# A four-layer network on one core: the order of work in the Mamba's opening, and a group norm cut into stages in the attention

## The chip, the cores and the metric

The kernel runs on one NeuronCore of a Trainium2 chip. A core has five engines that run side by side and wait for each other by semaphores: TensorE (matrix products, written to the PSUM memory), VectorE, ScalarE (activation functions, from tables that have to be loaded), GpSimd, and SyncE, which here only issues DMA transfers. In the profile they are PE (PEld for its weight loads), DVE, ACT, POOL and SP. [...] The metric is the device time of one execution in microseconds, as a median of several runs; lower is better.

## The reference

An image batch `x` of 2 × 128 channels × 56 × 56 pixels goes through four layers. Each has the form `x = x + layer(group_norm(x))`, the norm over 32 groups of 4 channels:

```
x = x + agent_attention(_gn(x))   # layer 0
x = x + conv3x3(_gn(x))           # layer 1
x = x + mixture_of_experts(_gn(x))# layer 2: 2x2 patches, 8 experts, the best 2 of each patch
x = x + mamba_pair(_gn(x))        # layer 3
```

Layer 0 replaces queries by mixtures of 49 agent vectors and then lets each of the 3136 pixels attend to all others, in 4 heads: `softmax(q_compressed @ k.T * scale) @ v`, then a projection and a layer norm. Layer 3 runs, over each image row of 56 pixels, a state-space recurrence forward and one backward. For each way:

```
xi, z = split(x @ in_w.T)
xc  = silu(conv_b + causal_conv4(xi))
dt, B, C = split(xc @ xproj_w.T)            # 8, 16 and 16 values per pixel
dt  = softplus(dt @ dt_w.T + dt_b)          # 256 channels
h_t = exp(dt_t * A) * h_(t-1) + (dt_t * xc_t) * B_t     # 16 states per channel
y   = (sum over states of h * C + xc * D) * silu(z)
```

The group norm itself: per channel a mean and a variance over the pixels, averaged over the four channels of a group, then `(x - mean) / sqrt(var + eps)`.

## The kernel before, in words

Everything is float32. The image stays in on-chip memory as `x[128, 2, 3136]` and is worked on in 7 blocks of 448 pixels per image (8 rows of 56). A version of the attention that is safe for extreme values stands behind a branch at the end and isn't entered for these inputs.

**The group norm** is a method of `Net`. VectorE has taken statistics of every block (`bn_stats`, L88). `group_norm` aggregates them (L94, `gn_mv`), has TensorE average them over groups by a product with a constant matrix (L96), fetches the means and forms a corrected variance (L98 to L102, `gn_q`), averages that over groups by a second product (L104), and takes the inverse root (`inverse_root`, L66 to L71): an addition on VectorE, Ln and Exp on ScalarE, three small VectorE operations.

**The attention** (`short_attention`) is a list of 14 blocks, image 0 and then image 1, each with 25 steps (key tiles of 128 pixels). Step i of a block computes the scores of one key tile for four heads (L584, `sc`), their exponentials (L587, `ex`, two ScalarE instructions of 128 × 896), adds these into a running sum on VectorE (L592 and L594, `ex_sum`), and multiplies an earlier tile's exponentials with the values (L602, `av`). `den` (L622) adds the sums up. The order on TensorE, ScalarE and VectorE is the order in which the program writes the instructions (`manual_schedule`). Besides, each step has room for one stage of other work. At fixed steps stages finish the block before (`after`: `divide` at 3 with a reciprocal of 2.95 us, `project` at 6, `measure` at 8 and so on) or prepare the next one (`ahead`: `q_scores` at 9, `q_softmax` at 11, `q_turn` at 15, `q_mix` at 18). In the steps left over, the list `rest` is worked off, one stage a step, from step 3 on (in the first block from the start). In it is the opening of the second image: seven `stats`, `norm`, then in turn `spread` of a block (VectorE: normalise, L110, and sum for the agents, L477) and `keys` of the same block (TensorE: L508 `k_ps`, ScalarE copies it, L509), at last agents and values. A stage may return a `fetch`, which is called at the start of the next step, ahead of that step's scores. In the block before the last (`n == len(blocks) - 2`), `rest` is the convolution's group norm and the seven `pad` stages that normalise image 0 for it. All score, key and norm tiles in PSUM come from one ring of three (`ps`, tag `sc`).

**The Mamba** (`mamba_pair`) works on 14 blocks as well. Each block has a forward and a backward half of 16 units (8 pairs of states by 2 halves of the 256 channels); a unit is an exponential `dA` on ScalarE (`decay`, L1656), a product `dBu` on GpSimd (`push`, L1667), a scan on VectorE (L1689), and later a product with C (L1695 on GpSimd or L1698 on VectorE) and a sum over states on TensorE. The preparation of the next block is booked in `agenda` at numbered steps of the loop: `run(step)` emits what is booked, `fetch(step + 1)` what it returned. For block 0 the steps are negative (`at = -32`), ahead of the loop: there is nothing else to do then, and the steps only set the order. In this part only ScalarE's order is that of the program; the other engines' order is chosen by a scheduler. The stages of a half are `conv` (L1545, then ScalarE `xc`, L1554), `silu` (loads a table, applies Silu, and loads the table for Exp and Ln back), `low` (L1574, copied at L1577), `send_low` (SyncE: to memory and back, spread over partitions, as `Bs` and `Cs`), `step` (L1597, four activations L1607 to L1611), `error`, `log`, `softplus` (L1627, L1628), `weigh` (GpSimd, L1632) and `send_steps` (SyncE: `dt2` and `dtu2`, L1644). Here all their PSUM tiles share the tag `mm`, which has one buffer.

Of the kernel before, what the change touches and what calls it, by code (L numbers as in the profile page):

```python
# [8 lines left out]
F32 = mybir.dt.float32  # L9
# [19 lines left out]
class Net:  # L29
# [57 lines left out]
            self.stats[b] = self.small.tile([P, NBLK, 6], F32, name=f"st{b}", tag=f"st{b}")  # L87
        self.nc.vector.bn_stats(self.stats[b][:, k, :], self.xb(b, k))  # L88

    def group_norm(self, b, pool, tag):  # L90

        nc, small = self.nc, self.small
        mv = small.tile([P, 2], F32, name="gn_mv", tag="gn_mv")
        nc.vector.bn_aggr(mv, self.stats[b].rearrange("p k s -> p (k s)"))  # L94
        ps = pool.tile([P, 512], F32, name="gn_ps", tag=tag)
        nc.tensor.matmul(ps[:, 0:1], self.group, mv[:, 0:1], start=True, stop=True)  # L96
        mean = small.tile([P, 1], F32, name="gn_mean", tag="gn_mean")
        nc.vector.tensor_copy(mean, ps[:, 0:1])  # L98
        d = small.tile([P, 1], F32, name="gn_d", tag="gn_d")
        nc.vector.tensor_sub(d, mv[:, 0:1], mean)  # L100
        q = small.tile([P, 1], F32, name="gn_q", tag="gn_q")
        nc.vector.scalar_tensor_tensor(q, d, d, mv[:, 1:2], ALU.mult, ALU.add)  # L102
        ps2 = pool.tile([P, 512], F32, name="gn_ps2", tag=tag)
        nc.tensor.matmul(ps2[:, 0:1], self.group, q, start=True, stop=True)  # L104
        rstd = small.tile([P, 1], F32, name="gn_rstd", tag="gn_rstd")
        self.inverse_root(rstd, ps2[:, 0:1])
        return mean, rstd

    def normed(self, out, in_, mean_rstd):
        self.nc.vector.tensor_scalar(out, in_, mean_rstd[0], mean_rstd[1], ALU.subtract, ALU.mult)  # L110
# [273 lines left out]
def short_attention(net, wide, conv):  # L384
# [20 lines left out]
    with ExitStack() as ctx:  # L405
# [56 lines left out]
            net.take_stats(m.b, k)  # L462

        def norm(m):
            m.norm = net.group_norm(m.b, banks, "mm")

        def spread(m, k):

# [231 lines left out]

        def opening(m):
            todo = [lambda k=k: stats(m, k) for k in range(NBLK)]
            todo.append(lambda: norm(m))
            for k in range(NBLK):
                todo += [lambda k=k: spread(m, k), lambda k=k: keys(m, k)]
            todo += [lambda: agents_of(m), lambda: agent_products(m)]
            if m is images[0]:

                first = [getattr(blocks[0], ahead[i]) for i in sorted(ahead)]
                v = values_of(m)  # L710
                todo += [v[0], first[0], v[1], v[2], first[1], v[3], first[2], v[4], first[3]]
            else:
                todo += values_of(m)
            return todo
# [17 lines left out]
        with tc.manual_schedule(engines={E.PE, E.Activation, E.DVE}):  # L732
# [10 lines left out]
            for n, blk in enumerate(blocks):  # L743
                if n == len(blocks) - 2:
                    pad = one.tile([P, PAD * PAD], F32, name="pad0", tag="xn0")
                    rest = [lambda: conv.norm(0, banks, "mm")]
                    rest += [lambda k=k: conv.pad(0, pad, k) for k in range(NBLK)]
                for i in range(STEPS):
                    for f in fetches:
                        f()  # L750
                    fetches = []
                    blk.score(i)
                    waiting.append((blk, i))
                    quota = 0 if i == 1 else 2 if i == 3 else 1
                    if n == 0 and i == 0:
                        quota = 0
                    for _ in range(quota):
                        if len(waiting) > 1:
                            who, at = waiting.pop(0)
                            fetches.append(who.average(at))  # L760
                    if i == 2 and prev:
                        prev.sum_up(len(ENDS) - 1)
                    if i - 2 in ENDS:
                        blk.sum_up(ENDS.index(i - 2))
                    stage = None
                    if i in after and prev:
# [52 lines left out]
class Conv3x3:  # L819
# [21 lines left out]
        return [lambda some=some: turn(some) for some in (range(0, 4), range(4, 8), range(8, 9))]  # L841

    def norm(self, b, ps, tag):
        self.norms[b] = self.net.group_norm(b, ps, tag)

    def pad(self, b, pad, k):

# [538 lines left out]
def mamba_pair(net, out, wts, combine):  # L1386
# [19 lines left out]
    with ExitStack() as ctx:  # L1406
# [125 lines left out]
        class Half:  # L1532
# [101 lines left out]
                at = 0 if self.w.d == "f" else HW - 1  # L1634
                nc.gpsimd.memset(self.dt.rearrange("p m (r t) -> p (m r) t", t=HW)[:, :, at : at + 1], 1e31)

            def send_steps(self):

                self.dt2 = work.tile([P, 2, 2, BLK], F32, name="dt2", tag="dt2")
                self.dtu2 = work.tile([P, 2, 2, BLK], F32, name="dtu2", tag="dtu2")  # L1640
                for to, src in ((self.dtu2, self.dtu), (self.dt2, self.dt)):
                    for s in range(2):
                        for r in range(2):
                            nc.sync.dma_start(to[s * H : (s + 1) * H, :, r, :], src[r * H : (r + 1) * H, :, :])  # L1644

            def unit(self, u):
                return u // 2, u % 2
# [81 lines left out]
        def book(step, *stages, tag="mm", late=0):  # L1729

            agenda.setdefault(step, []).extend((stage, tag, late) for stage in stages)

        for n, blk in enumerate(blocks):
# [3 lines left out]
            if n == 0:  # L1737
                book(at + 1, blk.norm)
                for i, (h, m) in enumerate(((f, 0), (f, 1), (b, 0), (b, 1))):
                    book(at + 4 + 2 * i, lambda h=h, m=m: h.conv(m))  # L1740
                    book((1, 4, 5, 13)[i], lambda h=h, m=m: h.gate(m))
                book(at + 14, lambda f=f: silu(f, None), lambda b=b: silu(b, None))
                book(at + 16, f.low)
                book(at + 17, f.send_low)
                for h, t in ((f, at + 16), (b, 0)):
                    for m in range(2):
                        book(t + 2 + 3 * m, lambda h=h, m=m: h.step(m))
                        book(t + 3 + 3 * m, lambda h=h, m=m: h.error(m))
# [115 lines left out]
def layers(tc, a, out, wide, attention):  # L1864
    with ExitStack() as ctx:
        net = Net(ctx, tc, a)
        keep = ctx.enter_context(tc.tile_pool(name="keep2", bufs=1, side="right"))
        with tc.tile_pool(name="l1_keep", bufs=1) as taps:
# [5 lines left out]
            with tc.tile_pool(name="l2_w", bufs=2) as wpool:  # L1874
                with tc.tile_pool(name="l1_ps", bufs=2, space=PSUM) as ps, tc.tile_pool(name="l1", bufs=2) as nat:
# [3 lines left out]
                    def convolved(b):  # L1879
                        if b in done:  # L1880
                            return
                        pad = wpool.tile([P, 4, 2048], F32, name=f"pad{b}", tag="w1").rearrange("p q f -> p (q f)")
                        pad = pad[:, : PAD * PAD]
                        conv.norm(b, ps, "mm")
# [52 lines left out]
```

## Time and profile before

| | us |
|---|---|
| median of 3 runs | 3184.22 (3183.93 to 3184.84) |
| the profiled execution | 3175.44, its span 3173.7 |
| attention, up to the first product of the convolution | 0 to 902 |
| convolution, routing | 902 to 1066 |
| experts | 1066 to 1712 |
| their results gathered, Mamba's opening | 1712 to 1808 |
| Mamba loop, from its first scan to the addition after the last products | 1808 to 3141 |

Times in the profile are microseconds from the start of the span. A row of the timeline has start, duration, engine, line, operation, result and sources, and in brackets the idle time of the engine before it and what ended that. Matmuls of float32 show as two records each, so `x8` is four matmuls. A row of the waits names who waited, on which line, for whom, and then the total, the number of times and the longest. TensorE's granted clock is 1.00 at full speed.

### The profile page before, as it was taken

Reading aid. Unit: us, or ns where it says so; the run is one execution under the profiler, and the core shown is the slowest. Engines: PE = TensorE matmul, PEld = TensorE weight load, DVE = VectorE, ACT = ScalarE, POOL = GpSimd, SP = SyncE. Lnnn points to the kernel's source line nnn. Section 1 sums busy time; section 2 is a strip of 40 time slices with the busy share of each in tenths; the row PEclk is TensorE's granted clock in tenths of the full one; section 3 lists DMA queues with packets and bytes.
Section 4 is the critical chain, followed back from the end, with each engine's and each line's share of the span. In section 5 each row is a group of like instructions: output and inputs, shape, how many; then the busy total and the mean of one; then the engine's idle time right before and its main releaser. Section 6 shows DMA issues by size and latency. Waiting matters only on the chain. (4 is left out here: it accounts for less than half of the span.)

```text
span 3173.7 us, 34586 instructions
## 1 busy us (share of the span) xinstructions
PE 2863.2 (90%) x13024; PEld 1091.1 (34%) x13024; DVE 2201.9 (69%) x1985; ACT 1752.3 (55%) x2618; POOL 1411.1 (44%) x755
## 2 busy tenths in 40 slices
PE   7899999998999799999995689998898988999985
PEld 3233333332344444444442223332233332233321
DVE  5788999998854211111112389999999999999997
ACT  5678878887720111111100367777777777777764
POOL 2000010000000000000002389999999999999996
PEclk9999999999998899999997698998999999898987
DMA  1000000000001687878755434454444354445350
GB/s 53 1 1 1 1 1 1 1 1 1 1 31 27 266 323 283 324 282 322 286 228 178 103 72 95 88 104 89 92 87 101 84 107 89 85 87 108 81 111 7
DMA packets 133397, 333.65 MB, mean 105 GB/s; under 512 B 20100, under 2 KB 90596, under 8 KB 129620
## 3 DMA queue, kind: packets, MB, share of 16 engines
q1 hardware_dynamic: 111616, 304.87, 33.5%
q0 software_dynamic: 5136, 14.70, 1.4%
q10 hardware_dynamic: 16452, 11.61, 1.1%
q8 instruction: 107, 1.75, 0.2%
q14 instruction: 86, 0.70, 0.1%
HBM read 262.56 MB, written 17.20 MB: 88 GB/s over the span
## 5 line engine op out<-in xcount | busy, mean ns | idle before, releaser
L1667 POOL TENSOR_TENSOR dBu<-dtu,Bs 128x896 f32<-128x896 f32 x448 | 923.2, 2087 | 72.2 <-DVE h L1689 52.2
L1689 DVE TENSOR_TENSOR_SCAN h<-dA,dBu 128x896 f32<-128x896 f32 x448 | 878.6, 2006 | 58.1 <-ACT dA L1656 56.5
L587 ACT ACTIVATE ex<-sc 128x896 f32<-128x896 f32 (+1 forms) x700 | 602.8, 917 | 111.1 <-PE sc L584 99.9
L594 DVE TENSOR_TENSOR ex_sum<-ex_sum,ex 128x1792 f32<-128x1792 f32 (+1 forms) x238 | 490.0, 2059 | 44.1 <-ACT ex L587 30.0
L1709 PE MATMUL y<-h,both 128*64 128x448 f32 x1792 | 474.5, 631 | 15.6 <-POOL h L1695 13.0
L584 PE MATMUL sc<-q,k 32*128 32x448 f32 (+1 forms) x2800 | 403.0, 589 | 3.6 <-ACT ex L587 2.9
L1208 PE MATMUL h_ps<-w,xs_c 128*128 128x512 f32 x896 | 392.0, 595 | 10.6 <-issue 9.9
L1656 ACT ACTIVATE dA<-dt,f_A 128x448 f32<-128x448 f32 x448 | 284.4, 637 | 110.3 <-DVE h L1689 76.8
L602 PE MATMUL av<-ex,va 128*32 128x448 f32 (+1 forms) x2800 | 335.0, 553 | 0.1
L1698 DVE TENSOR_TENSOR h<-h,c_ps 128x1792 f32<-128x1792 f32 x154 | 311.3, 2022 | 25.6 <-PE c_ps L1677 10.8
L549 POOL TENSOR_TENSOR a_e<-a_e,a_inv 112x784 f32<-112x784 f32 x14 | 41.6, 2973 | 644.1 <-ACT ex L587 436.5
L1656 ACT ACTIVATE dA<-dt,b_A 128x448 f32<-128x448 f32 x448 | 283.7, 636 | 62.9 <-DVE h L1689 50.0
L1212 DVE TENSOR_TENSOR he<-h_ps,sg 128x512 f32<-128x512 f32 x56 | 38.6, 691 | 397.0 <-PE h_ps L1208 374.3
L1159 POOL DMA_INDIRECT xr<-xd,whom x28 | 28.0, 998 | 593.8 <-PE xr_ps L1198 489.2
L1695 POOL TENSOR_TENSOR h<-h,Cs 128x1792 f32<-128x1792 f32 x70 | 279.1, 3986 | 3.2 <-DVE h L1689 2.8
L1677 PE MATMUL c_ps<-low,ident 40*64 40x448 f32 x616 | 173.2, 643 | 91.4 <-DVE h L1698 69.3
L1208 PEld LDWEIGHTS h_ps<-w,xs_c 128*128 128x128 f32 x896 | 168.5, 190 | 218.6 <-issue 201.9
L1709 PEld LDWEIGHTS y<-h,both 128*64 128x64 f32 x1792 | 117.9, 152 | 319.9 <-issue 248.4
L584 PEld LDWEIGHTS sc<-q,k 32*128 32x128 f32 (+1 forms) x2800 | 137.4, 181 | 231.1 <-issue 134.8
L1229 PE MATMUL o_ps<-w,ht 128*128 128x512 f32 x448 | 200.0, 599 | 8.0 <-DMA w<-in_L_conv_w_dram 8.0
L1231 ACT ACTIVATE ot<-o_ps,share 128x512 f32<-128x512 f32 x28 | 19.2, 688 | 287.0 <-PE o_ps L1229 287.0
L1211 ACT ACTIVATE sg<-h_ps 128x512 f32<-128x512 f32 x56 | 33.4, 597 | 256.8 <-PE h_ps L1208 256.8
(318 smaller groups left out, 3007.1 us busy)
## 6 DMA issues: line engine op xcount, KB each, us to landing
w<-in_L_conv_w_dram SPq DMA_DIRECT2D x28, 4096.0 KB, 19.5
w<-in_L_conv_w_dram SPq DMA_DIRECT2D x28, 2048.0 KB, 10.3
Bs<-far SPq DMA_DIRECT2D x56, 896.0 KB, 10.7
dtu<-sp_u SPq DMA_DIRECT2D x112, 224.0 KB, 3.9
dt<-dt SPq DMA_DIRECT2D x112, 224.0 KB, 5.2
Cs<-far SPq DMA_DIRECT2D x140, 112.0 KB, 7.5
os<-ot ACTq DMA_DIRECT2D x28, 256.0 KB, 7.8
xd<-xt SPq DMA_DIRECT2D x14, 224.0 KB, 2.8
```

What stands on the lines that cost most here:

```text
L584: nc.tensor.matmul(sc[:size, j, :BLK], self.m.k[rows, at : at + size], self.q[rows, :], start=True, stop=True)
L587: nc.scalar.activation(ex[:size, 2 * g : 2 * g + 2, :], sc[:size, :, :BLK], AF.Exp, scale=scale)
L594: nc.vector.tensor_add(self.total[g][:size], self.total[g][:size], ex[:size])
L602: nc.tensor.matmul(self.av[rows, :BLK], self.m.va[:size, i, rows], self.ex[i][:size, h, :], start=i == 0, stop=i == STEPS - 1,)
L1208: nc.tensor.matmul(h_ps, xc[:, q, :], w1[:, q, f0 : f0 + 512], start=q == 0, stop=q == 3)
L1229: nc.tensor.matmul(o_ps, ht[:, i, :], w2[:, i, :], start=i == 0, stop=i == nj - 1)
L1656: nc.scalar.activation(self.dA[u][:, r * BLK : (r + 1) * BLK], self.dt2[:, m, r, :], AF.Exp, scale=self.w.A[:, j, 2 * m + r : 2 * m + r + 1],)
L1667: nc.gpsimd.tensor_tensor(self.dBu[u], self.dtu2[:, m], self.B[:, j, :].unsqueeze(1).to_broadcast(shape), ALU.mult)
L1689: nc.vector.tensor_tensor_scan(hf, af, bf, 0.0, ALU.mult, ALU.add)
L1695: nc.gpsimd.tensor_tensor(h4, h4, c, ALU.mult)
L1698: nc.vector.tensor_tensor(h4, h4, c, ALU.mult)
L1709: nc.tensor.matmul(self.y[r * H : (r + 1) * H, m, :BLK], both, self.hc[j][:, m, r, :], start=False, stop=j == PAIRS - 1)
```

## The change

The group norm becomes three stages: `aggregate`, `means` and `deviations`; the last two return a fetch. Where it was called as a whole, a small loop calls the stages and their fetches one after the other, so that nothing moves there. In the attention, the second image's norm and the convolution's norm are put into `rest` as three stages. In the second image's opening, `keys(k)` comes after `spread(k + 1)`.

In the Mamba, for block 0 only, the forward way's Silu, `low`, `send_low` and steps are booked ahead of the backward way's second convolution, the backward Silu goes behind the forward way's transfers, and these are sent in two halves (first all that concerns the channels of m = 0, then those of m = 1), 16 transfers of 112 KB in place of 8 of 224 KB.

```diff
-    def group_norm(self, b, pool, tag):
+    def norm_stages(self, b, pool, tag, given):
...
+        def aggregate():
+            nc.vector.bn_aggr(mv, self.stats[b].rearrange("p k s -> p (k s)"))
+
+        def means():
+            ps = pool.tile([P, 512], F32, name="gn_ps", tag=tag)
+            nc.tensor.matmul(ps[:, 0:1], self.group, mv[:, 0:1], start=True, stop=True)
+
+            def fetch():
+                nc.vector.tensor_copy(mean, ps[:, 0:1])
+                d = small.tile([P, 1], F32, name="gn_d", tag="gn_d")
+                nc.vector.tensor_sub(d, mv[:, 0:1], mean)
+                nc.vector.scalar_tensor_tensor(q, d, d, mv[:, 1:2], ALU.mult, ALU.add)
+
+            return fetch
+
+        def deviations():
+            ps = pool.tile([P, 512], F32, name="gn_ps2", tag=tag)
+            nc.tensor.matmul(ps[:, 0:1], self.group, q, start=True, stop=True)
+
+            def fetch():
+                self.inverse_root(rstd, ps[:, 0:1])
+                given((mean, rstd))
+
+            return fetch
+
+        return aggregate, means, deviations
+
+    def group_norm(self, b, pool, tag):
+        got = []
+        for stage in self.norm_stages(b, pool, tag, got.append):
+            fetch = stage()
+            if fetch:
+                fetch()
+        return got[0]
...
             todo = [lambda k=k: stats(m, k) for k in range(NBLK)]
-            todo.append(lambda: norm(m))
-            for k in range(NBLK):
-                todo += [lambda k=k: spread(m, k), lambda k=k: keys(m, k)]
+            todo += [lambda stage=stage: now(stage) if m is images[0] else stage() for stage in norm(m)]
+
+            behind = 0 if m is images[0] else 1
+            for k in range(NBLK + behind):
+                todo += [lambda k=k: spread(m, k)] * (k < NBLK)
+                todo += [lambda k=k: keys(m, k - behind)] * (k >= behind)
...
-                    rest = [lambda: conv.norm(0, banks, "mm")]
+                    rest = conv.norm(0, banks, "mm")
...
-            def send_steps(self):
+            def send_steps(self, first=False):
...
-                for to, src in ((self.dtu2, self.dtu), (self.dt2, self.dt)):
-                    for s in range(2):
-                        for r in range(2):
-                            nc.sync.dma_start(to[s * H : (s + 1) * H, :, r, :], src[r * H : (r + 1) * H, :, :])
+                for some in (slice(0, 1), slice(1, 2)) if first else (slice(0, 2),):
+                    for to, src in ((self.dtu2, self.dtu), (self.dt2, self.dt)):
+                        for s in range(2):
+                            for r in range(2):
+                                nc.sync.dma_start(
+                                    to[s * H : (s + 1) * H, some, r, :], src[r * H : (r + 1) * H, some, :]
+                                )
...
-                    book(at + 4 + 2 * i, lambda h=h, m=m: h.conv(m))
+                    book(at + (3, 5, 8, 10)[i], lambda h=h, m=m: h.conv(m))
...
-                book(at + 14, lambda f=f: silu(f, None), lambda b=b: silu(b, None))
-                book(at + 16, f.low)
-                book(at + 17, f.send_low)
-                for h, t in ((f, at + 16), (b, 0)):
+
+                book(at + 7, lambda f=f: silu(f, None))
+                book(at + 9, f.low)
+                book(at + 11, f.send_low)
+                for h, t in ((f, at + 9), (b, 0)):
...
-                book(at + 25, f.weigh)
-                book(at + 25, f.send_steps)
+                book(at + 18, f.weigh)
+                book(at + 18, lambda f=f: f.send_steps(True))
+                book(at + 20, lambda b=b: silu(b, None))
```

More of the change, by code (lines that the diff above doesn't have):

```diff
@@ L88, in take_stats @@
         self.nc.vector.bn_stats(self.stats[b][:, k, :], self.xb(b, k))
-    def group_norm(self, b, pool, tag):
+    def norm_stages(self, b, pool, tag, given):
         nc, small = self.nc, self.small
         mv = small.tile([P, 2], F32, name="gn_mv", tag="gn_mv")
-        nc.vector.bn_aggr(mv, self.stats[b].rearrange("p k s -> p (k s)"))
-        ps = pool.tile([P, 512], F32, name="gn_ps", tag=tag)
-        nc.tensor.matmul(ps[:, 0:1], self.group, mv[:, 0:1], start=True, stop=True)
+        q = small.tile([P, 1], F32, name="gn_q", tag="gn_q")
@@ L97, in group_norm @@
         mean = small.tile([P, 1], F32, name="gn_mean", tag="gn_mean")
[L98 to L104, printed above, removed]
@@ L105, in group_norm @@
-        rstd = small.tile([P, 1], F32, name="gn_rstd", tag="gn_rstd")
-        self.inverse_root(rstd, ps2[:, 0:1])
-        return mean, rstd
+        rstd = small.tile([P, 1], F32, name="gn_rstd", tag="gn_rstd")
+        def aggregate():
[9 more added lines that the diff above has]
+            return fetch
@@ L464, in norm, with given, now @@
         def norm(m):
-            m.norm = net.group_norm(m.b, banks, "mm")
+            def given(norm):
+                m.norm = norm
+            return list(net.norm_stages(m.b, banks, "mm", given))
+        def now(stage):
+            fetch = stage()
+            if fetch:
+                fetch()
         def spread(m, k):
@@ L843, in norm, with given @@
     def norm(self, b, ps, tag):
-        self.norms[b] = self.net.group_norm(b, ps, tag)
+        def given(norm):
+            self.norms[b] = norm
+        return list(self.net.norm_stages(b, ps, tag, given))
     def pad(self, b, pad, k):
@@ L1883, in convolved @@
                         pad = pad[:, : PAD * PAD]
-                        conv.norm(b, ps, "mm")
+                        for stage in conv.norm(b, ps, "mm"):
+                            fetch = stage()
+                            if fetch:
+                                fetch()
                         for k in range(NBLK):
```

## The prediction

> **What bounds the kernel now.** First the page: its 40 slices of 79 us each, one row an engine (a digit is an engine's busy share in tenths).
>
> ```profile
> PE   7899999998999799999995689998898988999985
> DVE  5788999998854211111112389999999999999997
> POOL 2000010000000000000002389999999999999996
> ```
>
> In slices 0 to 11 (attention) TensorE is full, from 24 on (Mamba loop) GpSimd and VectorE are. The chain that ended last shows only the last 50 us, so I asked for waits by stretch. TensorE's from 60 to 195 us (us, times, longest):
>
> ```profile
> PE k_ps L508 <- DVE xn L110: 9.3, 4, 5.4
> PE gn_ps L96 <- DVE gn_mv L94: 4.3, 1, 4.3
> PE gn_ps L104 <- DVE gn_q L102: 0.8, 1, 0.8
> ```
>
> From 690 to 985 us the longest is the convolution's norm:
>
> ```profile
> PE gn_ps L96 <- DVE gn_mv L94: 7.2, 1, 7.2
> ```
>
> The table by stretches says whether such a wait costs time. Its columns: stretch, length, busy us of TensorE, its weight loads, VectorE, ScalarE, GpSimd, then TensorE's granted clock. First the stretch with the second image's opening, then a plain one.
>
> ```profile
> 74.00:137.00 63.00, 48.45 (x334) 15.59 (x330) 43.23 (x40) 35.11 (x46) 2.26 (x1) 0.89 0.00 1
> 200.00:270.00 70.00, 69.33 (x556) 23.40 (x556) 61.42 (x50) 55.83 (x70) 5.61 (x2) 1.00 0.00 1
> ```
>
> Plain, TensorE has no gap, so each gap is lost. The `att` copies (L613) agree: 58.58 us a plain block (249.12 to 307.70), 68.40 with the convolution's norm (776.37 to 844.77). TensorE's timeline (start, length):
>
> ```profile
> 78.55 0.56 PE L96 MATMUL gn_ps<-gn_mv,group 128*128 128x1 f32 x2 [4.25 <-DVE gn_mv L94]
> ...
> 80.38 1.87 PE L584 MATMUL sc<-q,k 32*128 32x448 f32 x8
> 82.19 1.72 PE L602 MATMUL av<-ex,va 128*32 128x448 f32 x8
> ...
> 131.62 1.83 PE L508 MATMUL k_ps<-xn,wk 128*128 128x448 f32 x2 [5.38 <-DVE xn L110]
> ```
>
> An `sc` group takes 1.03 us elsewhere, an `av` group 0.96: a long wait also has a slow restart. Then the Mamba's opening, ScalarE's timeline:
>
> ```profile
> 1766.75 0.64 ACT L1554 ACTIVATE xc<-conv_ps,c_L_conv_b_conv_b 128x448 f32<-128x448 f32 x1 [3.40 <-PE conv_ps L1545]
> 1767.40 1.28 ACT L1720 ACT_TABLE_LOAD   x1
> ...
> 1769.66 1.28 ACT L1723 ACT_TABLE_LOAD   x1
> 1770.95 1.28 ACT L1720 ACT_TABLE_LOAD   x1
> ...
> 1773.21 1.28 ACT L1723 ACT_TABLE_LOAD   x1
> 1774.51 0.53 ACT L1577 COPY low<-low_ps 40x448 f32<-40x448 f32 x1
> ```
>
> The forward way's second `xc` ended at 1759.31; `low`, which all its steps need, comes 15 us later, behind two backward convolutions, four table loads and two Silus. The chain runs on to SyncE's transfers and the first scan (1807.99):
>
> ```profile
> 1796.57 2.77 SPq L1644 DMA_DIRECT2D dtu<-sp_u  x4
> 1799.45 3.02 SPq L1644 DMA_DIRECT2D dt<-dt  x4
> ```
>
> [...] 1.87 for 1.03 us after 4.25 us idle, full length after 1.47. [...] Silu starts at 1768.69, as the load ends; I use 1.28. [...] the last issue ended at 1802.47 and what waited for it started at 1807.25.
>
> **Part 1, the second image's norm.** Before, one stage of step 14 puts both matmuls in TensorE's order, behind VectorE's 2 us sum. After, the aggregate alone is at step 14, the first matmul at 16 (15 is taken by `q_turn`), the second at 17, each fetch before the next step's scores. Laid out by the trace's durations from 74.30 (end of step 14's `av`): step 15 costs 1.03 + 0.96 + 0.87 + 0.97, ends 78.1; step 16 ends 80.1; `gn_mv` was ready at 78.4, so no wait, matmul to 80.6; step 17's scores and average to 82.5. Its matmul needs `gn_q`, which now stands behind the sums of steps 15 and 16: ScalarE's exponentials of 16 end at 80.85 (behind `et`, 0.9), VectorE's sum at 82.85, three small operations 0.55: 83.45. Wait 1.0; step 18 starts at 84.0. Before, it would have started at 89.4 (91.87 less the key matmul's 0.92 and its wait of 1.47). **Gain 5.4.** The fetch adds a wait: ScalarE's Ln stands behind VectorE's sum of step 17 (to 85.5), which idles ScalarE some 2.5 us with step 18's exponentials behind it, until 86.1. TensorE needs them at step 19, after its own 0.96 + 1.77 (`q_mix`): hidden, with about 0.3 us to spare. Without that cover it costs up to 2.5.
>
> **Part 2, keys one more stage behind.** The four waits were 1.47, 0.90, 1.53 and 5.38, and the last's slow restart cost 1.83 + 1.84 against 0.99 + 1.03: 1.65. A step is at least 1.9 us (an `sc` and an `av` group), more than each of the three short waits. The long one came from the reciprocal (2.95 + 3 × 0.55) at step 3 ahead of a spread at step 4. In the new order keys 2 stands at step 4 and keys 3 at step 7, with spreads done in the block before; spread 4, at step 5, is used only after step 9. **Gain 10.9**, residue set at 0, at most 2. VectorE stays the cover: its 43.2 us of the 63 must fit in about 47, 92%, a plain block's share (61.42 of 70 is 88%).
>
> **Part 3, the convolution's norm.** Steps 4, 5 and 7 in place of 4. The aggregate is ready at 792.0 as before, behind reciprocal and sum; TensorE comes to it one step later, at 786.8 instead of 784.9: wait 5.2 instead of 7.2, slow restart (1.5) stays. The second matmul, two steps on, finds its `q` (about 794.5 against 799) and saves its 0.79. **Gain 2.7.** The seven `pad` stages (0.51 VectorE) end later, still in the block before last: nothing.
>
> **Part 4, the Mamba's opening.** New ScalarE order: `xc` f0, f1, load, Silu f, load, `xc` b0, `low`, `xc` b1, steps; TensorE: conv f0, f1, b0, `low`, conv b1, `dt_ps`. All use one bank (`mm`, one buffer). From 1759.31: 1.28 + 0.95 + 1.28, ends 1762.86, while conv b0 ends at 1762.67; `xc` b0 to 1763.5; `low` matmul warm, four records of 0.46: 1765.4; copy 1766.0; conv b1 3.31, to 1769.35; `xc` b1 1770.0; `dt_ps` now warm (1.02 for 1.86), first softplus activation at 1771.1, before 1776.98. **Gain 5.9** for all behind it, T0 (the first transfer's issue) included: 1790.7. Of what moved: `send_low`'s nine DMAs leave SyncE 9 us earlier and land before T0; Silu b with two loads (3.5 us) goes behind the last `dt` copy, done at T0 + 1.4, where ScalarE idled 8.31 us; the other image's Ln and Exp wait behind it, for nobody before T0 + 8. If that cover went, it would cost 3.5.
>
> The split: 16 issues of 112 KB in place of 8 of 224 KB. Before, bytes set the pace (8 × 224 KB in 8.4 us, 213 GB/s), after, issue does: about 0.63 each (`Cs`, also 112 KB: 1.89 for three). First half: `dtu` landed at T0 + 5, `dt` at T0 + 7.7; the first scan T0 + 8.4, before 11.4. Second half: last issue T0 + 9.9, landed 12.6, second `dA` done 13.25, second scan 13.3, before 13.36. The backward `low` copy behind the third `dA`: 15.0 against 15.2. GpSimd's products come 1.3 late after the second, inside its own idle of 0.58 and 2.77 before 1833. **Net 0**, bounds -2 (landing slower) and +2 (early scan kept).
>
> **Sum.** 5.4 + 10.9 + 2.7 + 5.9 = 24.9 us. Against the profiled execution: 3175.44 - 24.9 = 3150.5. The median of the timed runs is 8.8 above that execution; I carry this over: 3184.2 - 24.9, **3159.3**.
>
> **Rivals.** *VectorE becomes the bound of the opening:* its sums lag by three steps, and the waits return at `gn_q`, keys or `den`. For it: 92% in that stretch, up to 2.95 us in one instruction. Against: plain blocks run so without waits. It would halve parts 1 and 2, 8 us: 3167. *The split send eats part 4:* the second half late, the backward way's steps with it, GpSimd stalled longer at 1856 (6.1 us already, on that way's transfer). For it: twice the issues. Against: the layout above. Loses 2 to 5: 3163. *More than summed:* the early scan kept, the conv norm's restart warm: 3153. *Slower:* TensorE's granted clock sags once the attention has no long pause. Place: attention, some 830 us; price 830 × (1/c - 1); above 0.2% slower from 31 us, c below 0.964; at c = 0.95 plus 44 less 25, 3203. Against: 1.00 in every plain block at 99% busy. *It doesn't do what it says:* the stages find no free step. Against: the built order shows every move; 3184.
>
> **How the numbers follow.** As summed 0.65 (own range 3154 to 3164), VectorE 0.13, split 0.11, more 0.06, slower 0.03, nothing 0.02. What a measurement of this kernel can tell from no change is about 0.2%, 6.4 us. Faster 0.95, same 0.02, slower 0.03. Range 3152 to 3169: VectorE's case is mostly inside, with the bounds of part 4.
>
> **What would show it.** Right: no wait `k_ps` <- `xn`; `gn_ps` <- `gn_mv` one wait of about 5 us; `gn_ps` <- `gn_q` about 1; the first `sp_e` 11.8 us after the end of the forward `xc`, before 17.7; the first scan some 9 us nearer to it, the second about 6. Wrong: `k_ps` waits over 2 us, an `sc` group that waits for ScalarE, a clock below 1.00 in plain blocks, or GpSimd's idle time before 1900 grown by what the opening won.

## The result, and the profile after

The changed kernel takes 3161.11 us (median of 4 runs, 3155.46 to 3161.96), the kernel before beside it 3184.3 (3183.93 to 3184.84): a ratio of 0.9922, 95% interval 0.9907 to 0.9938, or 23.2 us less. The prediction was 3159, in a range of 3152 to 3169. The profiled execution is one of the timed ones (3161.96, span 3160.2). In it the lines of the code are shifted: L508 became L541 (`k_ps`), L584 L617 (`sc`), L602 L635 (`av`), L94, L96, L102 and L104 of the norm L100, L104, L110 and L116, L1577 L1618 (`low`), L1644 L1686 (the transfers).

The page's slices, one row an engine:

```profile
PE   7999999999998899999985689898999899898985
DVE  5879989988954111111112479999999999999996
POOL 2000100100000000000003389999999999999995
```

The picture is the old one: TensorE bounds the attention, GpSimd and VectorE the Mamba loop. TensorE's waits from 60 to 195 us (total, times, longest) show what went:

```profile
PE g_ps L525 <- DVE agbd L518: 1.7, 1, 1.7
PE gn_ps L116 <- DVE gn_q L110: 0.7, 1, 0.7
PE sc L617 <- ACT ex L620: 0.5, 2, 0.2
```

The four `k_ps` waits (9.3 us) and the wait for `gn_mv` (4.3) are gone; a wait for `gn_q` of 0.7 is left; new is one of 1.7, in which the second image's agent products stand in TensorE's order before VectorE has scaled the agents. From 690 to 985 us:

```profile
PE gn_ps L104 <- DVE gn_mv L100: 5.2, 1, 5.2
```

The convolution's norm waits 5.2 us instead of 7.2, as its layout said. The stretches, with the same columns as before:

```profile
74.00:137.00 63.00, 62.11 (x478) 20.51 (x472) 57.00 (x58) 48.86 (x64) 3.08 (x1) 1.00 0.00 1
200.00:270.00 70.00, 69.33 (x559) 23.74 (x560) 61.33 (x55) 56.24 (x71) 8.53 (x3) 1.00 0.00 1
```

TensorE is busy 62.11 of the 63 us (48.45 before), VectorE 57.00 (43.23): 90%. It holds, with little left, and the clock granted to TensorE is 1.00 in both (0.89 before in the first, which held the long waits). ScalarE's timeline in the Mamba's opening:

```profile
1747.26 0.63 ACT L1595 ACTIVATE xc<-conv_ps,c_L_conv_f_conv_b 128x448 f32<-128x448 f32 x1 [3.40 <-PE conv_ps L1586]
1747.92 1.28 ACT L1764 ACT_TABLE_LOAD   x1
1749.21 0.95 ACT L1764 ACTIVATE xc<-xc 128x896 f32<-128x896 f32 x1
1750.18 1.28 ACT L1767 ACT_TABLE_LOAD   x1
1751.47 0.63 ACT L1595 ACTIVATE xc<-conv_ps,c_L_conv_b_conv_b 128x448 f32<-128x448 f32 x1
1753.89 0.53 ACT L1618 COPY low<-low_ps 40x448 f32<-40x448 f32 x1 [1.79 <-PE low_ps L1615]
...
1759.56 0.63 ACT L1648 ACTIVATE sp_e<-dt_ps,c_L_conv_f_dt_b 128x448 f32<-128x448 f32 x1 [1.10 <-PE dt_ps L1638]
```

`low` now comes 6.0 us after the forward way's last `xc` (which ends at 1747.89), and the first `sp_e` 11.67 us after it; before, 17.67. Then the transfers, on SyncE's queue, and VectorE's first scans:

```profile
1778.76 2.42 SPq L1686 DMA_DIRECT2D dtu<-sp_u  x4
1781.30 2.45 SPq L1686 DMA_DIRECT2D dt<-dt  x4
1783.79 2.53 SPq L1686 DMA_DIRECT2D dtu<-sp_u  x4
1786.42 2.46 SPq L1686 DMA_DIRECT2D dt<-dt  x4
```

```profile
1786.25 2.02 DVE L1733 TENSOR_TENSOR_SCAN h<-dA,dBu 128x896 f32<-128x896 f32 x1 [4.83 <-ACT dA L1700]
1791.38 5.85 DVE L1733 TENSOR_TENSOR_SCAN h<-dA,dBu 128x896 f32<-128x896 f32 x3 [3.11 <-ACT dA L1700]
```

With T0 for the first transfer's issue (1778.76), the first scan is at T0 + 7.5, the second at T0 + 12.6: before, 11.4 and 13.4. So far the prediction's sketch fits nearly step by step. But two stretches of this profile are longer than before, and neither was foreseen. One is TensorE in the first Mamba block, where the backward way's softplus begins:

```profile
1814.14 1.86 PE L1668 MATMUL sp_ps<-sp_u,ident 128*128 128x448 f32 x2 [2.98 <-ACT sp_u L1663]
1815.80 1.70 PE L1668 MATMUL sp_ps<-sp_e,minus 128*128 128x448 f32 x2
1817.29 1.70 PE L1668 MATMUL sp_ps<-dt,ident 128*128 128x448 f32 x2
1819.61 5.20 PE L1586 MATMUL conv_ps<-pad,f_conv_t 128*128 128x448 f32 x8 [0.62 <-ACT dt L1669]
```

The kernel before has the same gap of 2.98 us:

```profile
1832.67 1.02 PE L1627 MATMUL sp_ps<-sp_u,ident 128*128 128x448 f32 x2 [2.98 <-ACT sp_u L1622]
1835.82 3.31 PE L1545 MATMUL conv_ps<-pad,f_conv_t 128*128 128x448 f32 x8 [0.62 <-ACT dt L1628]
```

There the three products took 1.02, 0.92 and 0.91 us; here they took 1.86, 1.70 and 1.70, and the granted clock in the trace is 0.50 from 1813.26 to 1823.50. VectorE's read-out waits 7.59 us for `c_ps` behind them, where the kernel before had 3.37, and the backward way's own transfers are issued at T0 + 55.2 instead of T0 + 51.7. The other is the gather of the experts' outputs just ahead of the Mamba. From the aggregate of the statistics (L100) to the first padded copy passed 13.0 us, before 6.35, in VectorE's timeline:

```profile
1727.86 0.16 DVE L107 COPY gn_mean<-gn_ps 128x1 f32<-128x1 f32 x1 [2.95 <-remote]
...
1733.55 0.16 DVE L66 TENSOR_SCALAR ir_v<-gn_ps 128x1 f32<-128x1 f32 x1 [4.79 <-remote]
```

The releaser is given only as `remote`; the product that the second row reads had ended at 1729.2. Because of these two, and because the profiled execution of the kernel before (3175.44) was shorter than all its timed runs beside it, this pair of profiles differs by only 13.5 us, while the medians differ by 23.2. The questions for the chip: are the four parts worth what was predicted, do the two losses belong to the change, and can the waits that are left (5.2 and 1.7) be had too?

### The profile page after: what moved, and what is told of

It is laid out like the page before. It is cut to its first block, busy times and chain, and to the rows that moved or that the text cites. A ratio compares the mean times of both kernels' runs of the same rounds, so it can differ in the third digit from the quotient of the medians.

```text
span 3160.2 us, 34597 instructions
## 1 busy us (share of the span) xinstructions
PE 2864.5 (91%) x13024; PEld 1091.8 (35%) x13024; DVE 2200.8 (70%) x1985; ACT 1752.5 (55%) x2618; POOL 1411.3 (45%) x755
## 5 line engine op out<-in xcount | busy, mean ns | idle before, releaser
L1753 PE MATMUL y<-h,both 128*64 128x448 f32 x1792 | 474.4, 631 | 15.5 <-POOL h L1739 12.9
L617 PE MATMUL sc<-q,k 32*128 32x448 f32 (+1 forms) x2800 | 402.5, 586 | 3.6 <-ACT ex L620 2.9
L635 PE MATMUL av<-ex,va 128*32 128x448 f32 (+1 forms) x2800 | 334.3, 552 | 0.1
L1700 ACT ACTIVATE dA<-dt,b_A 128x448 f32<-128x448 f32 x448 | 283.7, 636 | 63.3 <-DVE h L1733 50.4
L617 PEld LDWEIGHTS sc<-q,k 32*128 32x128 f32 (+1 forms) x2800 | 137.7, 181 | 228.8 <-issue 129.5
L1252 ACT ACTIVATE sg<-h_ps 128x512 f32<-128x512 f32 x56 | 33.4, 597 | 257.4 <-PE h_ps L1249 257.3
```

Source lines behind the costliest of these rows:

```text
L617: nc.tensor.matmul(sc[:size, j, :BLK], self.m.k[rows, at : at + size], self.q[rows, :], start=True, stop=True)
L635: nc.tensor.matmul(self.av[rows, :BLK], self.m.va[:size, i, rows], self.ex[i][:size, h, :], start=i == 0, stop=i == STEPS - 1,)
L1700: nc.scalar.activation(self.dA[u][:, r * BLK : (r + 1) * BLK], self.dt2[:, m, r, :], AF.Exp, scale=self.w.A[:, j, 2 * m + r : 2 * m + r + 1],)
L1753: nc.tensor.matmul(self.y[r * H : (r + 1) * H, m, :BLK], both, self.hc[j][:, m, r, :], start=False, stop=j == PAIRS - 1)
```

## The experiments

Four sets, each on one chip, another for each set; the kernel before had medians of 3177.5 in the first, 3184.28 in the second, 3177.23 in the third and 3176.44 in the fourth. The expectations of the first set speak of a kernel before of 3184 us; so its times are read as differences to 3177.5.

**The attention alone** (the changed kernel with the Mamba's opening of before).

```diff
-                    book(at + (3, 5, 8, 10)[i], lambda h=h, m=m: h.conv(m))
+                    book(at + 4 + 2 * i, lambda h=h, m=m: h.conv(m))
...
-                book(at + 18, lambda f=f: f.send_steps(True))
+                book(at + 25, f.send_steps)
```

> The attention's half of the change alone (norm stages and keys behind), the Mamba's opening as before. Theory of the sum: its blocks win about 16 to 17 us, and this reaches the end whole: 3167 to 3169. Rival, that the Mamba's opening won nothing at the end and the attention brought all 23 us: 3161. Rival, that the attention's gain is partly given back by the stages behind it: 3172 or more.

Measured 3158.33 (3155.42 to 3160.6), ratio 0.9938 (0.9924 to 0.9952): 19.2 us less, more than the 16 to 17 expected here; the sum of parts 1 to 3 was 19.0. In the trace the first product of the 3x3 convolution starts at 883.52 instead of 901.88, 18.4 us earlier. VectorE did not become the bound: TensorE is busy 62.11 us of the stretch from 74 to 137. But the products in the first Mamba block are slow here too, and the backward transfers go at T0 + 56.2, so the agreement of the time with the 19.0 may be in part chance.

**The Mamba's opening alone** (the kernel before with part 4).

```diff
-                    book(at + 4 + 2 * i, lambda h=h, m=m: h.conv(m))
+                    book(at + (3, 5, 8, 10)[i], lambda h=h, m=m: h.conv(m))
...
-                book(at + 25, f.send_steps)
+                book(at + 18, lambda f=f: f.send_steps(True))
```

> The Mamba's opening alone, the attention as before. Theory of the sum: 5.9 us less, 3178 to 3179; the first sp_e stands 11.8 us after the end of the forward xc. Rival, that TensorE's slow restart in the first block (three softplus products at half clock, then the convolution) and GpSimd's idle time eat the opening's gain: 3182 to 3184, with the opening itself still 6 us shorter in the timeline.

Measured 3174.25 (3170.67 to 3184.73), ratio 0.9989 (0.9981 to 0.9997): 3.3 us less, not 5.9. The opening itself gave all it should (the first `sp_e` 11.67 us after the last forward `xc`), but the `sp_ps` products took 1.86, 1.70 and 1.70 us here too, and the backward transfers went at T0 + 55.3, much as the rival had it.

**The norm's stages without the keys** (the first kernel with the keys in their old place).

```diff
-            behind = 0 if m is images[0] else 1
+            behind = 0
```

> The norm's three stages alone; keys one stage behind spread and the Mamba's opening as before. Theory of the sum: parts 1 and 3, 5.8 + 2.1 = 8 us less, 3176; the k_ps waits for xn come back, about 9 us. Rival, that the stages only move the wait into the keys (VectorE late in the same way): 3180 or more.

Measured 3168.91 (3164.41 to 3173.05), ratio 0.997 (0.996 to 0.998): 8.6 us less, where parts 1 and 3 had been put at 8.1 (5.4 and 2.7). TensorE's waits from 60 to 195 us in this kernel:

```profile
PE k_ps L541 <- DVE xn L135: 7.8, 3, 5.4
PE g_ps L525 <- DVE agbd L518: 1.7, 1, 1.7
PE gn_ps L116 <- DVE gn_q L110: 0.7, 1, 0.7
```

The key waits are still here, and the norm's is not: the two edits act separately. By difference to the first kernel the keys are worth 10.6 us in time; predicted 10.9. By the first product of the convolution it is 10.9 (894.46 to 883.52), and this is the cleaner measure, since the first kernel's profile has the slow products and this one's has not (T0 + 52.0).

**Without the split of the first transfers.**

```diff
-                book(at + 18, lambda f=f: f.send_steps(True))
+                book(at + 18, lambda f=f: f.send_steps(False))
```

> The changed kernel with the forward way's steps sent in 8 transfers of 224 KB, not in 16 of 112 KB. Theory of the sum: the split is worth 0 (bounds -2 and +2), 3159 to 3163; the first scan 3 to 4 us later after the first issue, the second scan about the same. Rival, that the split carries the opening's gain: 3164 or more.

Measured 3148.16 (3147.36 to 3150.51), ratio 0.9908 (0.9893 to 0.9923): 29.3 us less than before, more than theory (21 to 25) or rival allowed. In its trace the first scan comes at T0 + 11.5 and the backward transfers at T0 + 51.65, with `sp_ps` at full speed. That looked as if the split cost more than it brings. But the first kernel, which has no split either, had the slow products. So the next set looked for the cause.

**The changed kernel again, and kept at work.** The second kernel was to have three idle products ahead of the backward way's first `sp_ps`, to keep TensorE at work in the gap.

```diff
             def softplus(self, m, keep=0):
                 pm = mm("sp_ps")
+                for _ in range(keep):
+                    nc.tensor.matmul(pm[:, :BLK], net.ident, self.dt[:, m, :], start=True, stop=True)
...
-                        book(t + 7 + m, lambda h=h, m=m: h.softplus(m))
+                        book(t + 7 + m, lambda h=h, m=m: h.softplus(m, 3 if h is b and m == 0 else 0))
```

> The changed kernel as it is, as the measure for the runs beside it. Theory (the half-speed product after the 2.98 us gap in the first Mamba block, and the 6.7 us that the first profile of it had in the gather of the statistics, are accidents of one execution): 23 us below the kernel before on the same chip, within 3; the gather stage at 6.3 us again; the backward way's first send of its steps either 51.7 us (products of 0.92) or 55.2 us (1.70) after the forward one. Rival (the split transfers bring the half-speed products with them): 55.2 us again.

> The changed kernel with three idle products (448 columns against the identity, their result overwritten) ahead of the backward way's first sp_ps in the first Mamba block, so that TensorE works through most of the 2.98 us in which it waits for the logarithm. Theory (TensorE at half speed after the gap is what the first Mamba block lost): sp_ps products at 0.92 us instead of 1.70, the convolution after them at 3.3 instead of 5.2, the backward way's first send 51.7 us after the forward one instead of 55.2, and 3.5 us less than the changed kernel where that one has the half-speed products. Rival (the split transfers themselves delay the backward way): the send stays at 55 us with the products at 0.92, and the time is that of the changed kernel or up to 2 us more for the idle products.

The changed kernel: 3155.54 (3152.26 to 3159.07), ratio 0.9909 (0.9891 to 0.9926); the gather's stretch 12.9 us again, against what was expected, and the backward transfers at T0 + 55.4, as the rival had it.

The edit of the second kernel does nothing: the stage runs later than it is booked, and `b` then names the last block's way, so that no idle product is issued. Its profile counts 13024 records of matmuls, as many as the changed kernel's. What it measured, 3157.3 (3155.18 to 3160.2), ratio 0.9914 (0.99 to 0.9928), is the changed kernel once more, and its profile is of use as such. TensorE's timeline:

```profile
1812.07 1.86 PE L1670 MATMUL sp_ps<-sp_u,ident 128*128 128x448 f32 x2 [2.98 <-ACT sp_u L1663]
1813.72 1.60 PE L1670 MATMUL sp_ps<-sp_e,minus 128*128 128x448 f32 x2
1815.16 0.92 PE L1670 MATMUL sp_ps<-dt,ident 128*128 128x448 f32 x2
1816.70 3.31 PE L1586 MATMUL conv_ps<-pad,f_conv_t 128*128 128x448 f32 x8 [0.62 <-ACT dt L1671]
```

The same program, and here full speed is back in the second group of products, the convolution takes 3.31 us instead of 5.20, and the backward transfers go at T0 + 52.8, 2.6 us earlier than in the execution beside it. So the slow products delay that way, and their number varies with the split as it is. Whether TensorE kept at work through the gap would be free of them wasn't tried.

**The convolution's norm with one empty stage**, so that its first product stands at step 7 instead of 5.

```diff
                     rest = conv.norm(0, banks, "mm")
+                    rest.insert(1, lambda: None)
```

> The changed kernel with one empty stage between the aggregate and the first product of the convolution's norm, which puts that product at step 7 of the block in place of step 5. Theory (VectorE reaches the aggregate 5.2 us late, and TensorE's restart after that wait costs 1.5): both go, the block with the norm takes 59 to 60 us in place of 66.3, 6 to 7 us less than the changed kernel. Rival (VectorE is the bound of these steps, so the 5.2 us turn up at the next product that needs it): the block shrinks by less than 2 us and another wait for VectorE, on ex or on the second product of the norm, takes the rest.

Measured 3157.94 (3152.32 to 3162.83), ratio 0.9909 (0.9893 to 0.9926), the same as the changed kernel beside it. TensorE's waits from 670 to 970 us:

```profile
PE sc L617 <- DVE ir_v L66: 2.4, 1, 2.4
PE sc L617 <- DVE gn_mean L107: 1.4, 1, 1.4
...
PE gn_ps L104 <- DVE gn_mv L100: 0.3, 1, 0.3
```

The wait of 5.2 us is gone and 3.8 us stand at `sc` instead, again for VectorE. The block (from one `att` copy to the next) takes 67.1 us; in three profiles of the changed kernel it took 66.3 to 67.2. The rival holds: in this block VectorE is behind, by the reciprocal and the sums, and moving the product only moves the place where TensorE meets it.

**All together, and the second image's agents one stage later.** The combined kernel has no split, the empty stage of the last kernel, and one more ahead of the agent products; a later one is the same without the empty stage in the convolution's norm. The idle products of which both expectations speak are not issued in them either, for the same reason.

```diff
-            todo += [lambda: agents_of(m), lambda: agent_products(m)]
+            todo += [lambda: agents_of(m)] + [lambda: None] * (m is not images[0]) + [lambda: agent_products(m)]
```

> The changed kernel without the split of the first transfers, with the three idle products, with the empty stage in the convolution's norm, and with one empty stage between the scaling of the second image's agents and the products that read them. Theory (the four are independent): attention 6 to 7 us shorter by the norm and 1.7 by the agents, the first Mamba block 3.5 shorter where the half-speed products would have come, so 8 to 12 us below the changed kernel, some 33 below the kernel before. Rival (VectorE as the bound of the attention): 3.5 us or less below the changed kernel.

> The changed kernel without the split, with the three idle products, and with the empty stage ahead of the second image's agent products; the convolution's norm as in the changed kernel. Theory (the agents' wait of 1.7 us is real, the convolution's norm indifferent): block 1 of the attention 2.8 us shorter and block 2 1.4 longer, the backward send at 51.8, 0.989 to 0.991 of the kernel before. Rival (VectorE's backlog takes it back later in the attention): the last block of the attention ends as late as in the changed kernel run without it.

Combined: 3156.07 (3153.55 to 3159.39), ratio 0.991 (0.9896 to 0.9925): not below the changed kernel of its set, as its rival had it. Agents later alone, in the third set: 3147.22 (3145.8 to 3152.09), ratio 0.9904 (0.9888 to 0.992). In both, the wait of 1.7 us at `g_ps` is gone, block 1 of the attention takes 63.3 us instead of 66.2 and block 2 64.9 instead of 63.5: 1.5 us net over these two. The backward transfers go at T0 + 51.8 and 51.6. The combined kernel's time doesn't show it. Against the profile of the changed kernel beside it, the backward transfers come 3.6 us earlier after T0; but the block with the convolution's norm takes 67.9 us instead of 67.2, the expert stage 810.4 instead of 809.6, and the stretch from the backward transfers to the last addition but one 1292.4 instead of 1289.7, together 4.2. Why that stretch was so short in the one execution isn't known. The kernel with the agents later has the lowest ratio of all, but its interval overlaps that of the changed kernel: that it is better is read from its trace, and not shown by its time.

**The kernel before, the one without the split, and the changed kernel, once more each.**

> The kernel before, unchanged, for a second profile of it. The first profile of the changed kernel and its four neighbours in the second set of runs spent 12 to 13 us between the aggregate of the image's statistics and the first padded copy of the Mamba stage, the first profile of the kernel before and the first set of runs 6.3. Theory (the stall belongs to the chip or the session, not to the change): the kernel before shows it too where the runs beside it do, and then takes some 6.5 us more than its first profile. Rival (the change causes it): 6.3 us here, and 12 to 13 in kernels with the changed opening beside it. Its ratio to itself is 1 within its interval. The backward way's first send at 51.7 us if TensorE is at full speed after its gap, 55 if not.

> The changed kernel without the split of the first transfers, a second time. Theory (the split costs nothing by itself, and TensorE's speed after its gap is an accident): 0.991 to 0.992 of the kernel before, as the changed kernel; the backward send at 51.7 or 55 us. Rival (the split puts TensorE into the slow phase): 51.7 again, and 3.5 us below the changed kernel's 0.991.

> The changed kernel a third time. Theory on the stall (it belongs to the chip or the session): on another chip than that of the second set, 6.3 us from the aggregate to the first padded copy in place of 12 to 13, and a time of 3152 to 3156; on the chip of the second set 12 to 13 again. Rival (the changed kernel brings it): 12 to 13 wherever it runs. Theory on the split (it brings the half-speed products): sp_ps at 1.70 us and the backward send at 55 us a third time. Rival (an accident of the clock's phase): 51.7 now and then.

The kernel before against itself: 1.0002 (0.9993 to 1.0012); backward transfers at T0 + 51.9; the gather's stretch 6.34 us. Without the split: 3151.51 (3146.37 to 3158.01), ratio 0.9921 (0.9904 to 0.9938); 51.7 and 6.34. The changed kernel a third time: 3152.47 (3151.44 to 3154.52), ratio 0.9929 (0.9912 to 0.9946); 55.3 and 6.35. In that execution of the changed kernel VectorE waits for nothing remote in the gather:

```profile
1722.16 0.16 DVE L107 COPY gn_mean<-gn_ps 128x1 f32<-128x1 f32 x1 [0.55 <-PE gn_ps L104]
1723.57 0.16 DVE L66 TENSOR_SCALAR ir_v<-gn_ps 128x1 f32<-128x1 f32 x1 [0.50 <-PE gn_ps L116]
```

The stall of the gather is thus not the change's alone: the same kernel has it or not. All four kernels of the second set have it and none of the other sets. The kernel before, too, is some 7 us longer in the two sets where it appears (3184.3 and 3184.28 against 3176.4 to 3177.5), though no profile of it from there exists, so that it stalls there too is likely and not shown. What VectorE waits for, 4 us after the product is done, is open.

The slow products go with the split nearly every time: TensorE's timeline in the third profile of the changed kernel, and then in the second of the one without the split.

```profile
1804.90 1.86 PE L1668 MATMUL sp_ps<-sp_u,ident 128*128 128x448 f32 x2 [2.98 <-ACT sp_u L1663]
1810.37 5.28 PE L1586 MATMUL conv_ps<-pad,f_conv_t 128*128 128x448 f32 x8 [0.62 <-ACT dt L1669]
```

```profile
1805.03 1.02 PE L1668 MATMUL sp_ps<-sp_u,ident 128*128 128x448 f32 x2 [2.97 <-ACT sp_u L1663]
1808.17 3.31 PE L1586 MATMUL conv_ps<-pad,f_conv_t 128*128 128x448 f32 x8 [0.62 <-ACT dt L1669]
```

All six profiles with the split begin this block slow (one recovers early), and of eight without it one does (the attention alone). The clock that each trace records shows where they differ. Two neighbouring stretches of 3.41 us around the gap, with the columns as above, first in the changed kernel, then without the split:

```profile
1800.77:1804.18 3.41, 1.16 (x8) 0.15 (x3) 1.63 (x2) 3.35 (x7) 2.47 (x2) 1.00 0.00 0
1804.18:1807.60 3.42, 2.69 (x4) 1.47 (x5) 3.42 (x3) 1.95 (x4) 2.42 (x1) 0.50 0.00 0
```

```profile
1800.29:1803.70 3.41, 1.76 (x9) 0.49 (x8) 1.23 (x3) 3.23 (x6) 2.09 (x1) 1.00 0.00 0
1803.70:1807.12 3.42, 2.09 (x6) 1.06 (x6) 3.42 (x3) 2.52 (x5) 1.82 (x1) 1.00 0.00 0
```

In these profiles the clock changes on a grid: in four stretches of the first one of the kernel before, all 36 changes, from 77 to 3149 us, lie whole multiples of 3.413 us apart, within 0.02. In all fourteen a tick of this grid falls inside the gap, at T0 + 34.5 to 35.5. Where TensorE had been idle for 2.07 to 2.59 of the 3.41 us before that tick, the clock fell to 0.50: in the six with the split, and at 2.07 in the attention alone. Where it had been idle for 1.60 to 2.01, the clock stayed: in the other seven. In the execution that recovers early, the first stretch behind that tick held 0.39 us of idle time, and the clock was back at its end; in the other six the first two held 0.62 us or more each, and it was back after the third. This is no rule for every place: behind the long gap that ends at T0 + 14.2 to 15.4 TensorE worked for over 9 us before the clock rose, at T0 + 24.3 to 25.3. The split's share is this: with it the gap begins at T0 + 32.4 to 32.8, without it at 33.0 to 33.4. Why the tick lies so nearly at one place after T0 is not known. That the earlier gap is what the split changes is read from these profiles; no run moved the gap alone.

In time the split's loss is not resolved: 0.9921 and 0.9908 without, 0.9922, 0.9909 and 0.9929 with.

## Why the prediction was right, step by step

The clean pair is the second profile of the kernel before (span 3174.8) and the third of the changed one (3151.3), neither with the gather's stall. From one to the other, in us (the last row ends at the addition of the last block but one to the image, which is also what stands at 3141 in the table of the kernel before; what follows takes 34.0 and 34.5):

| stretch | before | after | difference | predicted |
| --- | --- | --- | --- | --- |
| to the first product of the 3x3 convolution | 902.05 | 884.99 | -17.1 | -19.0 |
| routing and experts, to ScalarE's table load behind the last output copy | 813.20 | 809.59 | -3.6 | 0 |
| gather, norm, forward convolutions | 43.79 | 43.79 | 0.0 | 0 |
| end of the forward `xc` to T0 | 37.29 | 31.09 | -6.2 | -5.9 |
| T0 to the backward way's transfers | 51.91 | 55.33 | +3.4 | 0 |
| from there to the last addition but one | 1292.56 | 1291.98 | -0.6 | 0 |
| sum | | | -24.0 | -24.9 |

**Part 1, the second image's norm (5.4).** Right. In the kernel with the stages alone, the `att` copies to block 2 show it: 107.89 for 115.82, then 73.11 for 71.68 and 63.53 for 61.79, together 4.8 (the first copy itself varies between 102.8 and 105.3 in the profiles with the changed attention). `gn_q` was waited for 0.7 us (1.0 predicted); step 18 starts 9.3 us after the end of step 14's `av` (75.49 to 84.78 in the first profile of the changed kernel), where the layout had 9.7. ScalarE's Ln does stand behind VectorE for 2.45 us, and TensorE doesn't wait for it; the cover held. What the layout missed lies further back: the agents' scaling and the values behind it were moved with everything else, and TensorE waits 1.7 us for the first. Not moving that pair of stages apart cost 1.5.

**Part 2, the keys (10.9).** Right: 10.9 by the start of the convolution, 10.6 by time. By the `att` copies of the first and third kernels 4.6 in block 0 and 6.9 in block 1, 11.6; no residue.

**Part 3, the convolution's norm (2.7).** Half. Wait and slow restart are as laid out (5.21 us; `sc` 1.88 and `av` 1.72 after it), but from one `att` copy to the next the block takes 66.3 to 67.2 for 68.4: 1.2 to 2.1. The failed step is that a wait saved at the product is a gain: the kernel with the empty stage showed that VectorE is the limit there, as the first rival said for another place. Some 0.8 us came at the attention's tail.

**Part 4, the opening (5.9).** The opening's layout was right: 11.67 us for 11.8 to the first `sp_e`, 6.2 us with T0. The first scan is 10.3 us nearer to the last forward `xc` (some 9 predicted), the second 7.1 (some 6). The failed step is "split: net 0". It held up to T0 + 14 (the backward `low` copy is at T0 + 13.7, 1.0 earlier than before), and then 3.4 us were lost where nothing had been expected, at T0 + 35. The rival "the split send eats part 4: loses 2 to 5" had place and price nearly right (the backward way's steps late, 3.4 us) and the cause wrong: not late transfers, but TensorE at a clock of 0.50, which fell in a gap of 2.98 us. The prediction had reckoned with a slow restart only after longer gaps; in its own trace the products after this one took 1.02, 0.92 and 0.91 us. The sign that it named, GpSimd's idle time, is there in part: from T0 + 10 to T0 + 104 it grew from 11.7 to 14.2 us. (The pace of the old transfers is 218 GB/s rather than 213, with 224 KB as the profile counts them; nothing rests on it.) The gain at T0 was gone by more than half; 2.8 is left in this pair, 3.3 in the kernel with this part alone.

**The sum.** 24.9 us predicted, 23.2 measured. It is near partly by chance: of the 24.0 of the clean pair 3.6 are the expert stage, which reads 28 blocks of 4 MB and took 809.6 to 823.7 us in the profiles whatever the kernel; without it the parts give 20.4. The 8.8 us carried over from profile to median are for the most part, some 7, how the kernel before differs between sets of runs.

**The clock rival** (slower, 3203) fell: the granted clock is 1.00 in both stretches above, with TensorE busy 62.11 of 63 us.

## What to carry to other kernels

Where TensorE is full, a wait in its queue can be priced from its length and its slow restart, and splitting a chain into stages of the steps pays it back (the keys here: 10.9 us predicted, 10.9 measured); but ask first whether the engine waited for is only late in the order or behind in its work, since in the second case the wait moves to the next product (5.2 us at the convolution's norm became 3.8 us at `sc`). A short gap of TensorE on the critical path is worth a look even where it was harmless before: after 2.98 us of idle the same products took 0.92 or 1.70 us, by where the gap lay on the grid of 3.413 us on which the clock changed. And compare profiles stretch by stretch, so that a stretch that varies by itself isn't booked to the change.

## What the runs showed of the hardware

- After a gap of 2.98 us, TensorE's next 7 us of work ran with a granted clock of 1.00 in seven profiles and of 0.50 in seven, one of them for 3.4 us only; in the first pair of profiles the first product took 1.02 us and 1.86. The clock's changes lay on a grid of 3.413 us; at the tick in this gap it fell in the seven profiles with 2.07 to 2.59 us of idle time in the 3.41 us before, and stayed in the seven with 1.60 to 2.01. The backward transfers came at T0 + 55.2 to 56.2 where the clock stayed down for three stretches of 3.41 us, at T0 + 51.6 to 52.0 where it did not fall, and this stayed to the end (the stretch from the backward transfers to the last addition but one took 1289.7 to 1293.1 us in all fourteen profiles).
- The changed kernel spent 6.35 or 13 us in the same short chain of VectorE and TensorE beside indirect gathers, by the set of runs.
- Sixteen transfers of 112 KB were issued in 10.1 us (0.63 each), eight of 224 KB in 5.9; the first scan needs only half of them, and came 3.9 us earlier after T0.
